# The seam between two phases of a recommender kernel: query term, softmax denominator, exponentials and stores rearranged

## The chip, the cores and the metric

The kernel runs on one core of one Trainium2 chip. The metric is the device time of one execution in microseconds (us); smaller is better. The engines are called as in the profile: PE (TensorE, matmuls), PEld (its weight loads), DVE (VectorE), ACT (ScalarE), POOL (GpSimd) and SP (SyncE, which here only issues DMA transfers).

## The reference, cut to what matters

B is 1024 users, T is 100 steps, all widths are 128.

```python
def gru_step(h, x_t):                        # phase 1: h0 = 0, over 100 steps
    gi, gh = x_t @ gru_Wih.T + gru_bih, h @ gru_Whh.T + gru_bhh
    ...
    h_new = (1.0 - z) * n + z * h
keys = jnp.swapaxes(gru_seq, 0, 1)           # every h
q = jnp.broadcast_to(item_embedding[:, None, :], keys.shape)
feat = jnp.concatenate([keys, q, keys - q, q * keys], axis=-1)
score = _mlp(feat, [(att_W0, att_b0), (att_W1, att_b1), (att_W2, att_b2)], relu)
score = jnp.where(mask[:, :, None] == 1, score, -jnp.inf)
attn = softmax(score, axis=1)[..., 0]        # over the 100 steps
pooled = jnp.einsum('bt,btd->bd', attn, keys)
att_seq = pooled.T[:T]
def augru_step(h, inp):                      # phase 2: over the keys again
    x_t, a_t = inp
    ...
    u = a_t[:, None] * u
    h_new = (1.0 - u) * h + u * h_hat
attention_feature = aug_out[b, sequential_length[b] - 1]
comb = concat([user, item, hist_sum, item * hist_sum, attention_feature])
scores = _mlp(comb, [(ph_W0, ph_b0), (ph_W1, ph_b1), (ph_W2, ph_b2)], sigmoid)
```

The second recurrence needs the softmax over all 100 steps of the first, for its weight `a_t` is a row of `pooled` transposed. So the two phases run one after the other, with a seam where the softmax is finished, the pooled rows are stored and gathered again, and the second recurrence starts.

## The kernel before, in words

Everything is 32-bit floating point. The batch lies in the columns, in two halves of 512 (`HB`), so that a state is a tile of 128 x 512.

**Phase 1** (`gru_phase`) is a Python loop over the steps. In each step both halves do a GRU step (L534 matmuls, four column tiles of 32 at a time), and behind them the attention network works as a pipeline on the keys. `attend(t)` (L700) issues three layers at once on PE for both halves into one pair of PSUM banks `pm`: layer 1 of step t (weights `wk` and `wkq` on the state `hn` and on `kq`, the state times the item), and layers 2 and 3 of the two steps before it (weights `w12` on `mv`). `take(t)` evicts that: DVE adds the item's constant part `q0` to it (L734, tile `f`), ACT applies relu (L739) into `mv`. `q0` was made once by `item_part`, as `wq` times the item plus the biases `bm`. The layers after the last step, t = 100 and 101, have no first layer, and `take` applies relu with the bias straight from PSUM (L741). In `take`, row `SC` of `mv` is the score of step t-2, which two SP transfers per step bring into `s_b`.

**The softmax** is done block by block over the steps; the last blocks (`ENDS`) are 93 to 95, 96 to 97 and 98 to 99. A block has three stages, which `stage()` takes one after the other: `scores(0)`, `tops` (scores of half 1, L786 and L790, then maxima and subtraction, L794 to L800) and `sums` (mask L809, denominator L810 to L814). Between the second and the third stands the exponential on ACT (L806), issued by `exponents()`. In the seam (`banks` filled) the weights of the last two blocks are worked on in PSUM, and `sums` copies them to SBUF (L823) for POOL. `Half.pool(count, eng)` then multiplies keys by weights and adds them up (L626, L636, L637), on POOL for half 0 and on DVE for half 1.

**The seam** is written out by hand after the loop, from `gather_early(4)` on. It interleaves the attention layers of steps 98 and 99 and the two that follow, the `features` (`some(k)`: four matmuls each, L667, then a copy by ACT, L675, and one store of `part_d` per half), the softmax stages and the pooling. At its end DVE multiplies by `used` (L978) and stores to `pooled_d`: columns of steps 0 to 31 first (L982), the rest by SP (L987, half 1) and by ACT (L1410, half 0). The keys of the last rows are stored by `half.store` (L609), 1 MB per half.

A value loaded from DRAM then chooses one of three programs of **phase 2** by branches that every engine takes for itself. Phase 2 (`augru_phase`) works on users sorted by length. Key rows come by indirect gathers on POOL (L188; `load_row(1, 0, k)` for sixteen k, fourteen of them before the branch), the pooled rows by eight more (`gather_weights`, L153). PE transposes keys (L1110), makes the first step's gates (L1030), opens gates (L1127), spreads the first weights (L1053), and then `half_step` alternates between the halves, PE closing and opening gates (L1131, L1127).

There is no planner. Each engine runs its instructions in the order in which the code issues them, and waits for the others by semaphores.

Of the kernel before, what the change touches and what calls it, by code (L numbers as in the profile page):

```python
# [9 lines left out]
F32 = mybir.dt.float32  # L10
# [4 lines left out]
ALU = mybir.AluOpType  # L15
# [4 lines left out]
P = 128  # L20
B = 1024
T = 100
# [61 lines left out]
def kernel(ctx: ExitStack, tc: tile.TileContext, a: dict, out: bass.AP):  # L84
# [114 lines left out]
    def gru_phase(pools):  # L199
# [491 lines left out]
        def attend(t):  # L691

            p = left[t] = [pa.tile([P, HB], F32, tag="a", name="pm") for _ in halves]

            old = [half.mv if t else hist[:, half.cols] for half in halves]
            k_rows = slice(0 if t <= T else 2 * R, P)

            def pack(i, q, w, v, start, stop):
                s = ts(q, R)
                nc.tensor.matmul(p[i][s, :], lhsT=w[:, s], rhs=v, start=start, stop=stop)  # L700

            def first(i, q, j):
                if t < T:
                    w = (wk, wkq)[j][i]
                    pack(i, q, w, halves[i].first[t][j], j == 0 and q != QB[i], j == 1)

            def more(i, q):
                pack(i, q, w12[i][k_rows, :], old[i][k_rows, :], True, q == QA[i] or t >= T)

            for turn in range(2 * NH):  # L710
                i, j = divmod(turn, 2)
                for q in range(2):
                    first(i, q, j)
                if i == 0:
                    for q in range(2, P // R):
                        more((QA, QB)[j].index(q), q)
                else:
                    for q in range(2, P // R):
                        first(QB.index(q), q, j)
# [4 lines left out]
        def take(t):  # L724

            if t < 0:
                return
            p = left.pop(t)
            rows = slice(0 if t < T else 2 * R, P)
            sums = []  # L730
            for half in halves:
                if t < T:
                    sums.append(wp.tile([P, HB], F32, name="f"))
                    nc.vector.tensor_add(sums[-1], p[half.i], q0[:, half.cols])  # L734
            for half in halves:
                half.mv = wp.tile([P, HB], F32, name="mv", bufs=4)
                to, of, bias = half.mv[rows, :], p[half.i][rows, :], bm[half.i][rows, :]
                if t < T:
                    nc.scalar.activation(to, sums[half.i], AF.Relu)  # L739
                else:  # L740
                    nc.scalar.activation(to, of, AF.Relu, bias=bias)  # L741
            s, j = t - 2, soft["j"]
            if s < 0:
                return
            for half in halves:
                nc.sync.dma_start(
                    out=s_bs[NH * (j % 2) + half.i].rearrange("(p r) f -> p r f", r=R)[
                        :, s - blocks[j], :
                    ],
                    in_=half.mv[SC[half.i] : SC[half.i] + 1, :]  # L750
                    .unsqueeze(1)
                    .to_broadcast([1, P // R, HB]),
                )
            if s == blocks[j + 1] - 1:
                softmax()


        def softmax():

            j = soft["j"]  # L760
            b0, b1 = blocks[j], blocks[j + 1]
            n, last = b1 - b0, b1 == T
            rows = n + (1 if j else 0)
            on = later["on"][:, :, b0:b1]
            top_old, den_old = soft.get("top"), soft.get("den")
            e = sp.tile([P, NK, 2 * G + 1], F32, name="e", bufs=3)
            both = e, None
            if banks:

                b = banks["e"].pop()  # L770
                both = e, b[:, : NK * (G + 1)].rearrange("p (k n) -> p k n", n=G + 1)
                e = both[1]
                top_n, den_n = (b[:, NK * m : NK * (m + 1)] for m in range(G + 1, G + 3))
            top = sp.tile([P, NK], F32, name="top", bufs=3)
            den = sp.tile([P, NK], F32, name="den", bufs=3)
            if both[1] is None:
                top_n, den_n = top, den
            soft.update(j=j + 1, top=top, den=den, e=both)

            def scores(i):  # L780
                ks = ts(i, KH)
                if banks:
                    pt = blocked(banks["pt"])
                else:
                    pt = pa.tile([P, KH, R], F32, tag="a", name="pt")
                nc.vector.transpose(  # L786
                    pt, s_bs[NH * (j % 2) + i].rearrange("p (k r) -> p k r", r=R)
                )

                nc.vector.tensor_mul(e[:, ks, :n], pt[:, :, :n], on[:, ks, :])  # L790

            def tops():
                scores(1)
                nc.vector.tensor_reduce(top_n, e[:, :, :n], AX.X, ALU.max)  # L794
                if j:
                    nc.vector.tensor_max(top, top_n, top_old)
                    nc.vector.tensor_sub(e[:, :, n], top_old, top_n)
                    if both[1] is not None:
                        nc.vector.tensor_scalar_min(e[:, :, n], e[:, :, n], 0.0)
                nc.vector.tensor_sub(  # L800
                    e[:, :, :n], e[:, :, :n], top.unsqueeze(2).to_broadcast([P, NK, n])
                )
                soft["exp"] = exponents

            def exponents():
                nc.scalar.activation(e[:, :, :rows], e[:, :, :rows], AF.Exp)  # L806

            def sums():
                nc.vector.tensor_mul(e[:, :, :n], e[:, :, :n], on)  # L809
                nc.vector.tensor_reduce(den_n, e[:, :, :n], AX.X, ALU.add)  # L810
                if j:
                    old = sp.tile([P, NK], F32, name="old")
                    nc.vector.tensor_mul(old, den_old, e[:, :, n])
                    nc.vector.tensor_add(den, den_n, old)  # L814
                if last:
                    nc.vector.reciprocal(den, den)
                    nc.vector.tensor_mul(
                        e[:, :, :rows],
                        e[:, :, :rows],
                        den.unsqueeze(2).to_broadcast([P, NK, rows]),  # L820
                    )
                if both[1] is not None:
                    nc.vector.tensor_copy(both[0][:, :, :rows], e[:, :, :rows])  # L823
                for half in halves:
                    if j:
                        half.todo.append((both, n, None))
                    half.todo += [(both, t - b0, t) for t in range(b0, b1)]

            soft["stages"] += [lambda: scores(0), tops, sums]

        def stage(count=1):
            for _ in range(count):
                if soft["stages"]:
                    soft["stages"].pop(0)()
# [87 lines left out]
        def some(*these):  # L922
            for f in these:
                next(features[f])
# [6 lines left out]
        weights = soft["e"][0]  # L931
        exponents()
        some(0, 1)
        some(2, 3)
        take(T - 1)
        some(2, 3)
        attend(T)
        some(4)
        for half in halves:
            half.transpose(T - 1)  # L940
        stage()
        n = ENDS[-3] - ENDS[-4] + 1
        copy = banks["e"][0][:, : NK * n].rearrange("p (k n) -> p k n", n=n)
        nc.vector.tensor_copy(copy, weights[:, :, :n])
        for half in halves:
            half.todo = [
                ((w[0], copy if w[0] is weights else None), n, t) for w, n, t in half.todo
# [2 lines left out]
        halves[1].pool(1, nc.vector)  # L950
        stage()
        take(T)
        some(4)
        attend(T + 1)
        some(5, 6)
        stage()
        take(T + 1)
        exponents()
        some(5, 6)
        some(7)  # L960
        for half in halves:
            half.store((T - 1) // G)
        halves[1].pool(T, nc.vector)
        stage()
        gather_early(3)
        halves[0].pool(T, nc.gpsimd)
        some(7)
        stage(2)
        exponents()
        stage()  # L970
# [5 lines left out]
        for half in reversed(halves):  # L976
# [6 lines left out]
            later["att", half.i] = [  # L983
                (others[p - 1], t[p * R : (p + 1) * R]) for p in range(1, P // R)
            ]
        for to, t in later["att", 1]:
            nc.sync.dma_start(out=to, in_=t)  # L987

    def augru_phase(pools, widths, alive):

# [415 lines left out]
        gates = [first_step(i) for i in range(NH)]  # L1406
        for i in range(NH):
            load_key(1, i, (FREE_BANK, None)[i])
        for to, t in later["att", 0]:
            nc.scalar.dma_start(out=to, in_=t)  # L1410
        sorted_rows = [gather_weights(i) for i in range(NH)]
        for k in range(14, KH):
            load_row(1, 0, k)
        for i in range(NH):
            load_key(2, i, (FREE_BANK, None)[i])
# [11 lines left out]
        for t in range(1, T):  # L1427
# [6 lines left out]
            for i in range(NH):  # L1434
# [3 lines left out]
                    whole_step(t)  # L1438
                for _ in range(due.pop(0) if due else 0):
                    next(ahead, None)  # L1440
                if t > FIRST[1]:
                    next(more, None)
                if t == FIRST[2]:
# [113 lines left out]
```

## Time and profile before

| | us |
|---|---|
| median of 3 runs | 2017.4 (2016.58 to 2022.05) |
| the profiled execution, its own time | 2009.0 |
| its span in the profile | 2007.1 |
| PE busy | 1983.7 (99%) |
| DVE busy | 1671.7 (83%) |
| POOL busy | 1274.2 (63%) |
| ACT busy | 934.8 (47%) |
| phase 1's last matmul of a GRU step starts | about 1374 |
| phase 2 runs without a hole on PE from | 1432.9 |

The profile shows one execution. Its own time is 8.4 us below the median of the runs, so a sum worked out on the profile is a difference, to be taken from the median. Busy PE is not PE at its peak, but an idle PE is lost time wherever PE is the bound. A line in a timeline gives start, duration, engine, line, operation and tiles; a bracket at its end gives how long the engine was idle before it, and whose end released it. "issue" there means that the profile shows nothing that was waited for.

### The profile page before, as it was taken

What the parts mean: (1) busy time and instruction counts of PE and PEld (TensorE: products, weight loads), DVE (VectorE), ACT (ScalarE), POOL (GpSimd) and SP (SyncE); (2) the same over time, 40 slices, a digit from 0 to 9 for tenths busy, and PEclk for the clock granted to TensorE, in tenths of its full rate; (3) what the DMA queues carried; (4) which work ended last, traced back from release to release, by engine and by line L of the source; (5) the groups of instructions that cost most, each with busy time, mean ns of one, the idle gap of its engine ahead of it and who ended that gap; (6) DMA issues with size and microseconds to landing.
All of it is one profiled execution on the core that took longest, in us unless ns stands there. A gap on an engine that the chain in (4) does not pass through costs nothing. (4 is left out here: it accounts for less than half of the span.)

```text
span 2007.1 us, 41031 instructions
## 1 busy us (share of the span) xinstructions
PE 1983.7 (99%) x15380; PEld 994.6 (50%) x15380; DVE 1671.7 (83%) x3010; ACT 934.8 (47%) x1672; POOL 1274.2 (63%) x1325
## 2 busy tenths in 40 slices
PE   9999999999999999999999999998899999999998
PEld 2334444444444444444444444434444556678997
DVE  7878999887978888888878798998577777888985
ACT  4444454454544454544444454554343444444553
POOL 0233939669796959496896868898774353445331
PEclk9999999999999999999999999999999999999998
DMA  4443333333334434333333333333443343333331
GB/s 125 98 118 92 107 99 106 91 83 106 115 106 109 121 103 125 115 104 102 103 105 106 107 92 107 108 91 94 123 132 99 94 112 95 93 101 99 84 79 32
DMA packets 242075, 204.85 MB, mean 102 GB/s; under 512 B 59506, under 2 KB 204890, under 8 KB 241866
## 3 DMA queue, kind: packets, MB, share of 16 engines
q1 hardware_dynamic: 227514, 169.37, 30.2%
q0 software_dynamic: 12480, 32.04, 5.8%
q8 instruction: 123, 2.02, 0.4%
q10 hardware_dynamic: 1872, 0.72, 0.1%
q14 instruction: 86, 0.70, 0.1%
HBM read 146.01 MB, written 54.41 MB: 100 GB/s over the span
## 5 line engine op out<-in xcount | busy, mean ns | idle before, releaser
L534 PE MATMUL ps<-x,wih 128*32 128x512 f32 x4800 | 616.3, 593 | 0.0
L534 PE MATMUL ps<-hn,whh 128*32 128x512 f32 x4752 | 610.7, 592 | 1.4 <-ACT hn L582 1.4
L534 PEld LDWEIGHTS ps<-x,wih 128*32 128x32 f32 x4800 | 216.1, 110 | 302.0 <-issue 298.7
L534 PEld LDWEIGHTS ps<-hn,whh 128*32 128x32 f32 x4752 | 214.3, 110 | 298.9 <-issue 295.3
L519 POOL TENSOR_TENSOR xm<-x,m 128x512 f32<-128x512 f32 x200 | 234.9, 1174 | 143.2 <-DMA m<-mask_d 142.9
L546 ACT ACTIVATE r<-ps,brz 128x512 f32<-128x512 f32 x200 | 137.7, 689 | 386.3 <-PE ps L534 386.1
L520 POOL TENSOR_TENSOR hist<-hist,xm 128x512 f32<-128x512 f32 x200 | 257.9, 1290 | 15.7
L188 POOL DMA_INDIRECT rows<-keys_d,idx_k x218 | 211.5, 970 | 80.7 <-POOL rows L187 72.5
L637 POOL TENSOR_TENSOR pooled<-pooled,kw 128x512 f32<-128x512 f32 x191 | 245.0, 1283 | 15.0
L636 POOL TENSOR_TENSOR kw<-kt,e 128x512 f32<-128x512 f32 x191 | 206.2, 1080 | 69.7 <-DVE e L809 69.6
L565 ACT ACTIVATE ps<-ps,bih 128x512 f32<-128x512 f32 x200 | 132.4, 662 | 229.4 <-DVE ps L564 229.4
L700 PE MATMUL pm<-hn,wk 128*32 128x512 f32 x1200 | 221.8, 592 | 0.0
L700 PE MATMUL pm<-kq,wkq 128*32 128x512 f32 x1200 | 221.7, 592 | 0.0
L1139 ACT ACTIVATE c<-ph,bh 128x510 f32<-128x510 f32 (+57 forms) x174 | 88.3, 507 | 261.1 <-PE ph L1131 261.0
L554 DVE SCALAR_TENSOR_TENSOR u<-ps,bhh,r 128x512 f32<-128x512 f32 x198 | 147.5, 745 | 71.3 <-PE ps L534 68.6
L700 PE MATMUL pm<-mv,w 128*32 128x512 f32 (+1 forms) x808 | 195.4, 592 | 0.6 <-DVE e L790 0.6
L569 DVE TENSOR_TENSOR d<-hn,ps 128x512 f32<-128x512 f32 x198 | 136.1, 687 | 35.9 <-ACT ps L565 35.7
L564 DVE TENSOR_TENSOR ps<-ps,u 128x512 f32<-128x512 f32 x200 | 140.0, 700 | 25.9 <-remote 4.5
L582 ACT COPY hn<-ps 128x512 f32<-128x512 f32 x200 | 116.6, 583 | 93.5 <-DVE kq L576 91.8
L570 DVE TENSOR_TENSOR d<-ps,d 128x512 f32<-128x512 f32 x200 | 138.4, 692 | 26.0 <-ACT ps L566 11.6
L187 POOL COPY rows<-rest 128x1 f32<-128x1 f32 x202 | 38.4, 190 | 175.4 <-DVE rest L1168 170.0
L571 DVE TENSOR_TENSOR ps<-ps,d 128x512 f32<-128x512 f32 x200 | 139.9, 700 | 6.8
(224 smaller groups left out, 3111.8 us busy)
## 6 DMA issues: line engine op xcount, KB each, us to landing
x<-in_hist_x SPq DMA_DIRECT2D x210, 256.0 KB
keys_d<-kt SPq DMA_DIRECT2D x48, 1024.0 KB
m<-mask_d SPq DMA_DIRECT2D x200, 128.0 KB
rows<-keys_d,idx_k POOLq DMA_INDIRECT x218, 3.0
s_b<-mv SPq DMA_DIRECT2D x200, 8.0 KB
keys_d<-kt SPq DMA_DIRECT2D x32, 64.0 KB
mask_i<-in_mask SPq DMA_DIRECT2D x8, 200.0 KB
part_d<-part SPq DMA_DIRECT2D x2, 400.0 KB
```

The costliest lines, as they stand in the source:

```text
L188: nc.gpsimd.indirect_dma_start(out=r[:, at, :], out_offset=None, in_=keys_d[q], in_offset=bass.IndirectOffsetOnAxis(ap=idx_k[:, k, i : i + ...
L519: nc.gpsimd.tensor_mul(d, x, m)
L520: nc.gpsimd.tensor_add(acc, acc, d)
L534: nc.tensor.matmul(p[ts(q, R), :], lhsT=w[:, g, ts(q, R)], rhs=v, start=(j == 0), stop=(j == len(parts) - 1),)
L546: nc.scalar.activation(r, pr, AF.Sigmoid, bias=brz[:, 0:1])
L554: nc.vector.scalar_tensor_tensor(out=u, in0=ph, scalar=bhh[:, 2:3], in1=r, op0=ALU.add, op1=ALU.mult,)
L564: nc.vector.tensor_add(pi, pi, u)
L570: nc.vector.tensor_mul(d, pz, d)
L571: nc.vector.tensor_add(pi, pi, d)
L636: eng.tensor_mul(d, k, w)
L637: eng.tensor_add(acc, acc, d)
L700: nc.tensor.matmul(p[i][s, :], lhsT=w[:, s], rhs=v, start=start, stop=stop)
```

## The change

1. `attend` for steps 98 and 99 issues, for both halves, the query term too: `wq` on the item, six more matmuls of 32 columns per layer, summed up in `pm`. `take` for these steps drops the DVE addition and applies relu with the bias `bm` straight from PSUM.
2. In `sums` of block 93 to 95 the copy of the weights to PSUM comes ahead of the denominator, which is summed from the copy, and the temporary `old` lies in PSUM. The separate copy after the third stage goes.
3. The seam is put in another order: one feature less ahead of each of attend(100) and attend(101); `exponents()` of block 96 to 97 ahead of `take(101)`; half 1's pooling split so that more of it comes ahead of the last block's scores; POOL's second pooling ahead of the row gathers, which are two there instead of three; the keys' stores after the last feature, which puts them behind the second `part_d` store on SP.
4. The `pooled_d` stores of steps 32 to 99 (six transfers) are issued on SP in step t = 2 of phase 2, three after each half step, instead of three by SP at the end of phase 1 and three by ACT at the start of phase 2.
5. One key row gather more (three instead of two) comes after the pooled rows' gathers.

On the engines' queues: PE 12 matmuls more; DVE two pairs of additions less; ACT the same count without the three transfers; SP three transfers more.

```diff
@@ attend
+            def query(i, *groups):
+                for q in groups:
+                    pack(i, q, wq[i], item[:, halves[i].cols], False, False)
+
             for turn in range(2 * NH):
                 i, j = divmod(turn, 2)
+                if j and T - 2 <= t < T:
+                    query(i, 0, 1)
+                    if i:
+                        query(1, QB[1])
+                        query(0, QB[0])
                 for q in range(2):
                     first(i, q, j)
@@ take
-                if t < T:
+                if t < T - 2:
                     sums.append(wp.tile([P, HB], F32, name="f"))
                     nc.vector.tensor_add(sums[-1], p[half.i], q0[:, half.cols])
...
-                if t < T:
+                if t < T - 2:
                     nc.scalar.activation(to, sums[half.i], AF.Relu)
                 else:
                     nc.scalar.activation(to, of, AF.Relu, bias=bias)
@@ sums
                 nc.vector.tensor_mul(e[:, :, :n], e[:, :, :n], on)
-                nc.vector.tensor_reduce(den_n, e[:, :, :n], AX.X, ALU.add)
+                f, old = e, None
+                if banks and both[1] is None:
+                    b = banks["e"][0]
+                    f = soft["copy"] = b[:, : NK * rows].rearrange("p (k n) -> p k n", n=rows)
+                    old = b[:, HB - NK :]
+                    nc.vector.tensor_copy(f, e[:, :, :rows])
+                nc.vector.tensor_reduce(den_n, f[:, :, :n], AX.X, ALU.add)
                 if j:
-                    old = sp.tile([P, NK], F32, name="old")
-                    nc.vector.tensor_mul(old, den_old, e[:, :, n])
+                    if old is None:
+                        old = sp.tile([P, NK], F32, name="old")
+                    nc.vector.tensor_mul(old, den_old, f[:, :, n])
                     nc.vector.tensor_add(den, den_n, old)
@@ the seam
         some(0, 1)
-        some(2, 3)
+        some(2)
         take(T - 1)
-        some(2, 3)
+        some(2)
         attend(T)
-        some(4)
+        some(3)
...
-        n = ENDS[-3] - ENDS[-4] + 1
-        copy = banks["e"][0][:, : NK * n].rearrange("p (k n) -> p k n", n=n)
-        nc.vector.tensor_copy(copy, weights[:, :, :n])
+        copy = soft["copy"]
...
         take(T)
-        some(4)
+        some(3)
         attend(T + 1)
-        some(5, 6)
+        some(4, 5)
         stage()
+        exponents()
         take(T + 1)
-        exponents()
-        some(5, 6)
-        some(7)
+        some(4, 5)
+        some(6, 7)
+        halves[1].pool(1, nc.vector)
+        stage()
+        halves[0].pool(T, nc.gpsimd)
+        gather_early(2)
+        halves[1].pool(2, nc.vector)
+        some(6, 7)
         for half in halves:
             half.store((T - 1) // G)
-        halves[1].pool(T, nc.vector)
-        stage()
-        gather_early(3)
-        halves[0].pool(T, nc.gpsimd)
-        some(7)
         stage(2)
         exponents()
...
-        for to, t in later["att", 1]:
-            nc.sync.dma_start(out=to, in_=t)
@@ augru_phase
-        for to, t in later["att", 0]:
-            nc.scalar.dma_start(out=to, in_=t)
         sorted_rows = [gather_weights(i) for i in range(NH)]
-        for k in range(14, KH):
+        for k in range(13, KH):
             load_row(1, 0, k)
...
+                if t == FIRST[1] - 2:
+                    for to, of in later["att", i]:
+                        nc.sync.dma_start(out=to, in_=of)
```

## The prediction

> **What bounds the kernel now.** The page's first part comes first: TensorE (PE) is busy nearly all the time, so time can only be won where it is not.
>
> ```profile
> PE 1983.7 (99%) x15380; PEld 994.6 (50%) x15380; DVE 1671.7 (83%) x3010; ACT 934.8 (47%) x1672; POOL 1274.2 (63%) x1325
> ```
>
> Next the table by stage tells where the missing per cent lies: PE (first number after the stretch) is full before 1373 us and after 1433 us, and has its holes in between, where the two phases meet and where the whole edit lies.
>
> ```profile
> 1345.00:1373.00 28.00, 28.00 (x264) 10.24 (x260) 25.95 (x41) 14.91 (x24) 25.17 (x23) 1.00 0.25 73
> 1373.00:1400.00 27.00, 25.82 (x162) 14.90 (x154) 23.47 (x47) 11.85 (x24) 23.14 (x21) 1.00 0.19 57
> 1400.00:1433.00 33.00, 22.34 (x87) 12.59 (x88) 17.25 (x39) 11.21 (x18) 23.77 (x24) 0.84 0.47 118
> 1433.00:1460.00 27.00, 27.00 (x73) 12.79 (x74) 19.37 (x32) 10.05 (x16) 20.19 (x36) 1.00 0.56 170
> ```
>
> So 11.8 us of idle PE are all that can be had. The chain of waits says which wait ends last there: the eighth gather of the pooled rows, then half 1's first state, then PE without a hole to the end.
>
> ```profile
> 1427.23 3.61 DMA att_r<-pooled_d,idx
> ...
> 1431.41 0.71 DVE spare L1064
> ...
> 1432.15 0.70 DVE h_all L1065
> ...
> 1432.89 1.12 PE pr L1131 x2
> ```
>
> The timelines of the engines show what stands just behind that gather, and what leads to it.
>
> ```profile
> 1389.31 1.02 DVE L813 TENSOR_TENSOR old<-den,e 128x32 f32<-128x32 f32 x1
> 1390.37 1.29 DVE L814 TENSOR_TENSOR den<-den,old 128x32 f32<-128x32 f32 x1
> ...
> 1400.16 0.19 DVE L813 TENSOR_TENSOR old<-den,last 128x32 f32<-128x32 f32 x1
> ```
> ```profile
> 1405.47 1.94 PE L1110 MATMUL pk<-ident,rows 128*128 128x128 f32 x8 [6.10 <-issue]
> 1409.13 2.07 PE L1030 MATMUL pu<-k,wu 128*128 128x512 f32 x2 [1.73 <-ACT k L1111]
> ...
> 1424.92 1.16 PE L1053 MATMUL first<-ident,att_r 128*128 128x128 f32 x8 [0.72 <-ACT k L1111]
> ```
> ```profile
> 1403.73 0.23 ACT L806 ACTIVATE last<-last 128x96 f32<-128x96 f32 x1 [4.00 <-DVE last L800]
> 1408.01 1.07 ACT L1111 COPY k<-pk 128x512 f32<-128x512 f32 x2 [4.04 <-PE pk L1110]
> ```
> ```profile
> 1411.35 1.27 POOL L637 TENSOR_TENSOR pooled<-pooled,kw 128x512 f32<-128x512 f32 x1
> ...
> 1418.45 0.95 POOL L153 DMA_INDIRECT att_r<-pooled_d,idx  x1 [2.17 <-DMA pooled_d<-s_b]
> ```
>
> Two chains run to 1432.89. The **data chain**: DVE and POOL finish the softmax and pooling (1414.12 with the last product, L978), the store lands, POOL issues eight gathers at 1.25 us. The **start chain** of the second phase: PE leaves the branch at 1405.47, ACT at 1408.01, and PE works through keys and first gates until 1424.92. Without the gather's wait half 1's weight row (`spare`, PE 1429.94 to 1431.37) would end about 0.4 us sooner; the two chains are that close.
>
> **What the Trainium skill says.** *Runtime: NRT & Kernel Launch*, Instruction fetch mechanics: a taken branch whose target is outside the fetched window forces a DMA fetch first. The trace agrees that the branch costs: PE 6.10 us, ACT at most 4.05 (its last exponential ends at 1403.96). POOL's pause is 2.17. *SBUF — State Buffer*, SBUF: two separate sides: DVE with two SBUF inputs and GpSimd exclude each other for a whole instruction. The trace agrees: L813 with both inputs in SBUF took 1.02 us, ending just after POOL's multiply (1389.19, 1.07 long); with one in PSUM 0.19. *TensorE: Matmul & The Clock Gate*, Part 3: column tiles run side by side, but matmuls start in order. The trace agrees: passes of 0.59 us start every 0.107 us.
>
> **The change part by part.**
>
> *Query on PE.* Each of attend(98) and attend(99) gets six more matmuls. Sixteen take 3.43 us (1346.89 to 1350.32), so six take 1.29 if the four column groups stay full; two of them fall on groups 0 and 1 alone, an extra round of 0.43 more. I take 1.72 each, 3.43 in all. In return DVE loses two pairs of L734 adds (about 1.2 each), and ACT waits for PE instead of DVE. Step by step, before in brackets: attend(98) ends about 1379.5 [1377.8]; `mv` of 98 at 1380.2 to 1381.4, behind the state's copy [1382.69], each activation at 0.63 as the 64-row ones of L741 (bound above 0.69, L546's); features 0 and 1 take 2.9, to 1382.5 [1381.61]; attend(99) 5.15, read from 1388.1 [1386.46, by DVE]; `mv` of 99 ends 1389.35 [1388.42]. So layer 99 is **0.9 later**, not earlier.
>
> *Denominator by PSUM.* L813 and L814 fall from 2.31 to twice 0.19: 1.9 us off DVE; the copy L944 only moves. DVE's start on block 93-95 is 1.2 earlier, and the exponential follows: sums done at about 1386.8 [1391.86], one key pooled to 1388.9.
>
> *Where that stall goes.* Block 96-97 needs `mv` of 99 in `s_b`. Its two SP issues take 0.5 each; landing I take as 2.5, as of the `att_r` gathers (2.4 to 2.6); bounds 1.5 to 3.5, since this trace never lets DVE wait for it. That is 1391.3 and 1391.9, so DVE, five us ahead, now idles 2.4. Then its own 3.04 of scores and maxima: 1394.4 [1396.94].
>
> *Exponentials ahead.* exp of 96-97 at 1394.5 on ACT, then `mv` of take(101), for which attend(101) is ready at about 1394.6 since one feature fewer stands before it: ends 1396.0 [1396.49]. Queued behind it: the feature copies. Behind the maxima DVE has one key (1.45), sums (1.1), two keys (3.6), then scores of 98-99 (3.0): exp at **1403.45** [1403.73]. The pooling put ahead uses up nearly all that was won. Sums 1.95, then seven operations instead of ten, 4.95: 1410.6 [1412.80].
>
> *POOL.* Block 93-95 ends 1394.9; without the three row gathers it waits for block 96-97's weights until 1396.9, five operations of 5.9 to 1402.7, two gathers 2.5, weights of 98-99 at 1405.7, 5.9 to 1411.5 [1412.62]. The last L978 product ends 1412.2 [1414.12], **1.9 earlier**. Three gathers (3.8) and the branch's 2.17 lead to 1417.4; the store, if 4.2 from issue to release again, to 1416.4. So the eight gathers start at 1417.4, 1.0 earlier (up to 2.0 if the pause was all store), and the last lands at 1429.8 [1430.84]. One gather more stands after them (1.25 on POOL), before paced ones that wait for `rest` at 1434: covered.
>
> *Start chain.* Features 4 to 7 now all follow attend(101): PE is through at 1400.1 [1399.37], and leaves the branch at 1406.2 at the same 6.1. ACT leaves it at 1407.7. Both still give the keys' copies 0.2 to 0.3 sooner: `first` at 1424.7, half 1's row from 1429.7, and with 1.05 for its eight passes DVE starts at about 1430.7 [1431.41]. PE pr at **1432.2, 0.7 us sooner**.
>
> *Stores put off.* The keys' two stores (1 MB each) go behind the second `part_d`, from 1397.1 to about 1401. The six `pooled_d` stores (SP 1.88, ACT 1.69 of issue) leave 1414 to 1418 for step t=2, about 1443. On ACT this frees nothing that PE waits for: PE runs gate openings until 1422. On SP they stand before `at` of (4,1), wanted a step later; DVE waits once for rows there (1.10 at 1460.08) under a full PE. I take 0; bounds -1.5 (the first stores land sooner alone) to +1.5 (rows late).
>
> Sum: 0.7 off, on a span of 2007.1 and its own time of 2009.0. The median of the runs shown is 2017.4 (2016.58 to 2022.05), 8.4 above; I subtract from the median: **2016.7**.
>
> **Rivals.** *Faster:* PE's 6.10 is fetch behind the keys' stores, and goes with them. For it: the DMA engines are full from 1398.8 to 1408.4. Against: ACT's branch at 1403.7 then lies in the stores instead, and the gathers bind after about 1.7 us. 2015.7.
> *No change:* `s_b` lands later than 2.5, exp of 98-99 slips past 1403.73, and the start chain loses what the gathers win. 2017.4.
> *Slower:* the keys' stores drain too late. They share SP's queue with the first `pooled_d` stores. At the trace's 9.6 us they drain at 1411, and the stores come at 1411.3 and 1412.2. From a drain after about 1413.2 the gathers slip with it, after 1414.2 they are later than now. A drain at 1417 costs 2.5 us: 2019.9. For it: 1 us of room; against: the rate is measured.
>
> **How the numbers follow.** Chances: forecast 0.50, faster rival 0.20, no change 0.15, slower 0.15. A measurement of this kernel tells about 0.3% from no change, 6.05 us, half of all idle PE in the stage. Faster by that much 0.12 (a quarter of the faster rival, the rest scatter of runs and what I have not seen), slower 0.08 (a third of the slower rival, and scatter), within 0.80. The unknowns reach from -3 to +3 us and the runs themselves spread 5.5: 2011.5 to 2020.5.
>
> **What would show it.** Right: L813 and L814 at 0.19 in block 93-95; DVE idle some 2.4 us before the transposes of 96-97; `mv` of 99 ending near 1389.3; exp of 98-99 near 1403.5; the eight gathers from 1417.4; half 1's pr at 1432.2. Wrong: PE out of its branch below 1404, or the gathers after 1418.5.

## The result, and the profile after

Over 14 executions each on one chip the changed kernel took 2021.78 us (2019.05 to 2025.22) and the kernel before 2019.01 us (2016.58 to 2022.05): a ratio of 1.0014, interval 1.0007 to 1.0021. It is slower by some 2.8 us; two repetitions gave 1.0015 each (below). The profiled execution has a span of 2019.5 us and an own time of 2021.3 us.

The first part of the page shows PE as busy as before:

```profile
PE 1989.4 (99%) x15404; PEld 985.9 (49%) x15404; DVE 1668.6 (83%) x3006; ACT 934.2 (46%) x1672; POOL 1274.9 (63%) x1325
```

In the table by stage (length, then busy time of PE, PEld, DVE, ACT and POOL, then granted clock, DMA share, GB/s) PE has lost its hole before 1400 us, and the one after it has grown:

```profile
1345.00:1373.00 28.00, 28.00 (x264) 10.28 (x260) 26.03 (x41) 15.02 (x24) 25.18 (x23) 1.00 0.25 75
1373.00:1400.00 27.00, 27.00 (x187) 14.93 (x180) 22.38 (x51) 11.87 (x23) 23.92 (x23) 1.00 0.12 39
1400.00:1433.00 33.00, 19.12 (x72) 10.93 (x71) 11.22 (x27) 9.53 (x16) 24.11 (x23) 0.77 0.44 119
1433.00:1460.00 27.00, 25.87 (x72) 12.71 (x73) 16.33 (x26) 9.81 (x15) 13.95 (x24) 0.90 0.50 136
```

The timelines of DVE, PE, ACT and POOL, one after the other, at the places that the prediction named:

```profile
1386.73 0.20 DVE L829 TENSOR_TENSOR last<-den,last 128x32 f32<-128x32 f32 x1
1386.96 0.19 DVE L830 TENSOR_TENSOR den<-den,last 128x32 f32<-128x32 f32 x1
...
1390.99 0.73 DVE L795 STREAM_TRANSPOSE last<-s_b 128x512 f32<-128x512 f32 x1 [1.92 <-DMA s_b<-mv]
```
```profile
1402.94 1.06 PE L1123 MATMUL pk<-ident,rows 128*128 128x128 f32 x8 [2.27 <-issue]
1410.73 2.07 PE L1043 MATMUL pu<-k,wu 128*128 128x512 f32 x2 [6.73 <-ACT k L1124]
```
```profile
1402.76 0.23 ACT L815 ACTIVATE last<-last 128x96 f32<-128x96 f32 x1 [1.72 <-DVE last L809]
1409.60 1.07 ACT L1124 COPY k<-pk 128x512 f32<-128x512 f32 x2 [6.61 <-issue]
```
```profile
1416.08 0.95 POOL L153 DMA_INDIRECT att_r<-pooled_d,idx  x1 [0.36 <-issue]
```

The softmax work went as planned, and so did the gathers, which start at 1416.08 instead of 1418.45. But ACT now stands still for 6.61 us between its last exponential and its first key copy, where it stood for 4.05, while PE's pause, 6.10 before, shrank to 2.27. PE has the first keys ready at once and then waits 6.73 us for ACT. The chain of waits has left the gathers and runs through ACT:

```profile
1402.76 0.23 ACT last L815
1402.99 0.42 ACTq L1497
1403.53 6.00 issue
1409.67 0.42 issue
1410.09 0.60 ACT k L1124
...
1431.99 0.70 DVE first L1077
1432.72 0.70 DVE h_all L1078
...
1440.80 1.12 PE pr L1144 x2
```

From the start of attend(98) to half 1's pr, the stage in which the whole edit lies, this execution took 66.02 us (1374.78 to 1440.80), the one before 58.54 (1374.35 to 1432.89). Not all of these 7.5 us belong to the change: a second profile of the same program (e14, below) has 59.32.

### The profile page after: what moved, and what is told of

It is laid out like the page before. It is cut to its first block, busy times and chain, and to the rows that moved or that the text cites. A ratio compares the mean times of both kernels' runs of the same rounds, so it can differ in the third digit from the quotient of the medians.

```text
span 2019.5 us, 41068 instructions
## 1 busy us (share of the span) xinstructions
PE 1989.4 (99%) x15404; PEld 985.9 (49%) x15404; DVE 1668.6 (83%) x3006; ACT 934.2 (46%) x1672; POOL 1274.9 (63%) x1325
## 4 chain that ended last, share of the span: by engine, by line
PE 95%; DVE 2%; issue 1%; ACT 1%; DMA 1%; SPq 0%; ACTq 0%; DVEq 0%
PE ps L534 49%; PE pm L700 17%; PE ph L1144 4%; PE pr L1144 4%; PE ph L1140 4%; PE pu L1144 4%; PE pu L1140 4%; PE pr L1140 4%; PE pr L1217 0%; PE ph L1217 0%; DMA item<-in_item 0%; PE spare L1066 0%; PE p L1304 0%; PE p L1345 0%; PE pu L1217 0%
## 5 line engine op out<-in xcount | busy, mean ns | idle before, releaser
L534 PE MATMUL ps<-x,wih 128*32 128x512 f32 x4800 | 788.8, 592 | 0.0
L534 PE MATMUL ps<-hn,whh 128*32 128x512 f32 x4752 | 782.9, 592 | 1.4 <-ACT hn L582 1.4
L534 PEld LDWEIGHTS ps<-x,wih 128*32 128x32 f32 x4800 | 236.3, 110 | 306.8 <-issue 277.9
L534 PEld LDWEIGHTS ps<-hn,whh 128*32 128x32 f32 x4752 | 234.3, 110 | 302.0 <-issue 294.9
L700 PE MATMUL pm<-hn,wk 128*32 128x512 f32 x1200 | 260.2, 592 | 0.0
L700 PE MATMUL pm<-kq,wkq 128*32 128x512 f32 x1200 | 260.1, 592 | 0.0
L700 PE MATMUL pm<-mv,w 128*32 128x512 f32 (+1 forms) x808 | 242.4, 592 | 1.4 <-DVE e L799 1.4
```

Of the source, the lines that this page charges most:

```text
L534: nc.tensor.matmul(p[ts(q, R), :], lhsT=w[:, g, ts(q, R)], rhs=v, start=(j == 0), stop=(j == len(parts) - 1),)
```

## The experiments

All times below from a profile are counted from the start of attend(98), since executions drift apart by a microsecond or two before it. "Exit" is the start of ACT's first key copy (`k<-pk`). One column comes from the DMA view: the pages of program that the engines fetch appear there as packets of kind "instruction", and cutting the time around the branch into steps of 0.2 us shows when. The figures here and in the table give the start of the step, so a packet can come up to 0.2 us later. In all 17 profiles a packet of about 8 KB on the queue q14 starts 1.7 to 2.1 us ahead of ACT's exit, and a packet of 16 KB on q8 starts 2.5 to 3.2 us ahead of PE's first transpose in phase 2. The records don't name the engine that a packet is for; that the distance is so nearly the same in every kernel is what ties the one to ACT and the other to PE. The second column gives the time at which the issue of the keys' stores starts.

| kernel | keys' stores issued, us | last exponential ends | then until the packet | ACT's exit | half 1's pr | its distance from the exit | ratio to before |
|---|---|---|---|---|---|---|---|
| before | 22.8 | 29.6 | 2.2 | 33.7 | 58.5 | 24.9 | 1 |
| after | 26.8 | 28.2 | 4.6 | 34.8 | 66.0 | 31.2 | 1.0014 |
| e5, after again | 26.8 | 28.2 | 4.7 | 34.9 | 65.2 | 30.3 | 1.0015 |
| e14, after, third | 26.8 | 28.2 | 4.6 | 34.6 | 59.3 | 24.7 | 1.0015 |
| e1 | 22.3 | 28.2 | 3.2 | 33.4 | 58.6 | 25.2 | 0.9994 |
| e2 | 26.8 | 28.2 | 4.8 | 34.8 | 60.5 | 25.7 | 1.0009 |
| e3 | 27.1 | 30.3 | 5.5 | 37.6 | 63.3 | 25.7 | 1.0014 |
| e4 | 25.9 | 29.6 | 3.4 | 34.8 | 59.7 | 24.8 | 1.0001 |
| e12, e4 again | 25.8 | 29.6 | 3.2 | 34.6 | 59.3 | 24.7 | 1.0004 |
| e11 | 25.9 | 29.6 | 3.4 | 34.7 | 59.6 | 24.8 | 1.0004 |
| e6 | none here | 28.3 | 1.6 | 31.7 | 61.1 | 29.4 | 0.9994 |
| e7 | none here | 31.2 | 1.4 | 34.3 | 62.0 | 27.7 | 0.9996 |
| e8 | 15.1, by ACT | 29.8 | 1.3 | 33.1 | 63.0 | 29.9 | 1.0005 |
| e9 | 15.5 | 29.9 | 1.3 | 32.9 | 58.2 | 25.3 | 1.0001 |
| e10 | 26.8 | 26.9 | 3.0 | 31.8 | 57.5 | 25.6 | 0.9994 |
| e13 | 15.5 | 30.8 | 1.2 | 34.0 | 58.8 | 24.8 | 0.9994 |
| e15 | 22.4 | 27.0 | 3.9 | 32.7 | 58.1 | 25.5 | 0.9999 |

The kernel before took 2008 us beside e1 to e4 and e9 to e15, and 2019 us beside the first comparison and e5 to e8; e5 to e8 ran on another chip than the other experiments. The profile of the kernel before is of the first kind, that of the changed kernel ("after") of the second.

### First round: which part costs

Two theories stood against each other. Stores: put off, the keys' 2 MB fall into ACT's way through the branch. Rest: something else of the change costs.

**e1_keys_back**, the changed kernel with these stores at their old place:

```diff
         take(T + 1)
+        for half in halves:
+            half.store((T - 1) // G)
         some(4, 5)
...
         some(6, 7)
-        for half in halves:
-            half.store((T - 1) // G)
```

> The changed kernel with one edit undone: the keys' two last stores stand again right behind take(101), ahead of the second part_d store on SP. Theory S (stores in the branch): in the changed kernel these 2 MB fill the DMA engines from about 1402 to 1410 us, while ACT fetches phase 2 behind its branch (6.6 us against 4.05), PE waits and its clock falls; with the stores back near 1397 the ACT pause falls to about 4 us and the time to 2017 to 2019, ratio to before 0.999 to 1.000. Theory P (pooled stores in phase 2) and theory Q (query matmuls on PE): no change from the changed kernel, ratio 1.0010 to 1.0018.

Measured 0.9994 (0.9985 to 1.0002): the loss is gone. ACT's pause is 5.16, PE's 4.18. So, in the changed kernel, putting the stores off is needed for the loss.

**e2_pooled_back**, the changed kernel with the six pooled stores where they were:

```diff
+        for to, t in later["att", 1]:
+            nc.sync.dma_start(out=to, in_=t)
...
+        for to, t in later["att", 0]:
+            nc.scalar.dma_start(out=to, in_=t)
```

> The changed kernel with the six pooled_d stores of steps 32 to 99 back at their old places (three by SP at the end of phase 1, three by ACT at the start of phase 2). Theory P: they delay the weight and row loads of phase 2 when issued in step 2; undone, the time falls by the 2.8 us lost, ratio 0.999 to 1.0003. Theories S and Q: ratio stays 1.0010 to 1.002, or rises by up to 1 us since the six stores stand beside the gathers again.

Measured 1.0009 (1.0001 to 1.0018), between the two kernels; it tells little by itself.

**e3_no_query_on_pe**, the changed kernel with DVE adding the query term again:

```diff
-                if j and T - 2 <= t < T:
+                if False:
...
-                if t < T - 2:
+                if t < T:
```

> The changed kernel with the query term of layers 98 and 99 added by DVE again (no extra matmuls, relu without bias from the sum). Theory Q: the 2.6 to 3.4 us of matmuls lie on the path, so the ratio falls to 0.999 to 1.0003. Theories S and P: within 1 us of the changed kernel, 1.001 to 1.002, because DVE waits for s_b anyway.

Measured 1.0014 (1.0008 to 1.0021): the query on PE is not what costs. ACT's timeline in this kernel has the longest pause of all:

```profile
1403.24 0.23 ACT L815 ACTIVATE last<-last 128x96 f32<-128x96 f32 x1 [3.42 <-DVE last L809]
1410.81 1.07 ACT L1124 COPY k<-pk 128x512 f32<-128x512 f32 x2 [7.33 <-POOL kw L636]
```

The POOL multiply named there can hardly be the releaser: here it is the second of its block, in e1 the first, and in e6 the copy (1405.81) starts before the first multiply of that block (1405.86). Elsewhere the same wait is put down to "issue". The packet is what fits in all of them. Against this, e3's time is no longer than the changed kernel's, though its exit is 2.8 us later; more on that below.

**e4_keys_put_off_alone**, the kernel before with the stores put off and nothing else:

```diff
         some(7)
-        for half in halves:
-            half.store((T - 1) // G)
...
         some(7)
+        for half in halves:
+            half.store((T - 1) // G)
         stage(2)
```

> The kernel before with one edit only: the keys' two last stores put off behind the last feature and the second part_d store. Theory S: this alone makes it slower, ratio 1.001 to 1.002, with PE's branch pause down to 2 to 3 us and ACT's up to 6 or more. Theories P and Q: ratio 0.9995 to 1.0005.

Measured 1.0001 (0.9993 to 1.0008): a miss for the stores theory. The pauses moved the way it said (ACT 4.05 to 5.23, where it named 6 or more, PE 6.10 to 2.64), the time did not. Put off by themselves, the stores make no loss that this comparison can tell.

### Second round: without the stores

**e5_after_again** is the changed kernel itself.

> The changed kernel as it is, beside the kernel before on this chip. All theories: ratio 1.0010 to 1.002. Theory S (the keys' stores in flight lengthen the instruction fetch behind the branch): ACT's pause between its last exponential and its first key copy is 6 us or more, PE's pause behind its features 2 to 3. Theory C (PE's clock falls by chance of its windows): the ratio and the pauses are not tied to each other.

Measured 1.0015 (1.0009 to 1.0021).

**e6_after_no_late_keys** and **e7_before_no_late_keys**: no store of the last key rows at the seam, in the changed kernel and in the one before.

```diff
                 elif n == G - 1 and t < T - 1:
                     self.store(q)
+                    if q == (T - 1) // G - 1:
+                        self.store(q, 1)
...
-        for half in halves:
-            half.store((T - 1) // G)
```

> The changed kernel without the two late key stores: the last four steps' key rows are filled from the four steps before, together with those, within the loop (so the output is not the reference's). Theory S: with quiet DMA engines ACT's pause falls from 6.6 to 2 to 3 us, PE's stays near 2.2; the gathers' wait ends last again; 4 to 5 us faster than the changed kernel, ratio to before 0.998 to 0.9993. Theory C: no better than the changed kernel by more than 1 us, ratio 1.0005 to 1.002.

> The kernel before with the same edit: no late key stores, the last four steps' rows filled early from the four before (output not the reference's). Theory S: PE's pause falls from 6.1 and ACT's from 4.05 to 2 to 3 us each, but the gathers still start at about 1418 behind POOL's and DVE's pooling, so little of it reaches the end: ratio 0.9985 to 1.0000. Theory C: 0.9995 to 1.0005 with the pauses unchanged.

Measured 0.9994 (0.9986 to 1.0003) and 0.9996 (0.9988 to 1.0004). With the DMA engines quiet, ACT's pause is 3.38 and 3.06, PE's 2.06 and 2.96. ACT in e6:

```profile
1402.20 0.23 ACT L817 ACTIVATE last<-last 128x96 f32<-128x96 f32 x1 [1.74 <-DVE last L811]
1405.81 1.07 ACT L1124 COPY k<-pk 128x512 f32<-128x512 f32 x2 [3.37 <-issue]
```

Here the two kernels cost the same. So the rest of the change, without the late stores, makes no loss that can be told either; it takes both together. The kernel e7 is no clean control, though: its last exponential came 1.6 us later than in the kernel before.

**e8_keys_early_by_act**, the changed kernel with the stores on ACT's queue, right behind the last transposes, instead of behind the last feature:

```diff
             half.transpose(T - 1)
+            half.store((T - 1) // G, nc.scalar)
```

> The changed kernel with its two late key stores issued by ACT right behind the last transposes (about 1390 us) instead of by SP behind the last feature (1401). Theory S: the 2 MB are through by about 1400, both pauses are 2 to 3 us, ratio 0.998 to 0.9995, less up to 1 us if the issues hold up ACT's layer 100 or the score rows wait among the stores. Theory C: as the changed kernel, 1.0005 to 1.002.

Measured 1.0005 (0.9997 to 1.0013), undecided. The pause is short, 3.24, but the last exponential comes 1.6 us later than in the changed kernel.

### Third and fourth round: order and stores, each both ways

**e9_keys_early_by_sp**, the changed kernel with the stores on SP right behind the loads of `s_b` for layer 99, instead of behind the last feature:

```diff
             half.transpose(T - 1)
+        for half in halves:
+            half.store((T - 1) // G)
         stage()
```

> The changed kernel with the two stores of the last key rows on SP right behind the loads of s_b of layer 99 (about 1390.5 to 1394), so that their 2 MB are through by about 1402, before ACT's last exponential. Theory branch (ACT's leaving of the branch waits for its program to be fetched behind whatever data is in flight): ACT's pause at its first key copy falls from 6.6 to between 3.1 and 4.0 us, PE's stays 2 to 3, and the time goes from 1.0015 to between 0.9985 and 0.9998 of the kernel before. Rival (the loss lies in the new order of exponentials and pooling, not in the stores): ACT's pause falls, but the time stays at 1.001 to 1.002. What may spoil it: s_b of layers 98 to 101 shares the DMA engines with the stores, and the last exponential comes up to 2 us later.

Measured 1.0001 (0.9993 to 1.0009). The pause fell to 3.03 as expected, the time less than expected; what the text gave as a spoiler came true, the last exponential is 1.7 us later.

**e10_old_order_keys_late**, the changed kernel with the order of exponentials and poolings of the one before, the stores still late:

```diff
-        exponents()
         take(T + 1)
+        exponents()
         some(4, 5)
         some(6, 7)
-        halves[1].pool(1, nc.vector)
+        halves[1].pool(T, nc.vector)
         stage()
-        halves[0].pool(T, nc.gpsimd)
         gather_early(2)
-        halves[1].pool(2, nc.vector)
+        halves[0].pool(T, nc.gpsimd)
```

> The changed kernel with the order of exponentials, key poolings and row gathers of the kernel before; query on PE, the denominator by PSUM and both kinds of stores put off stay. Theory branch: the late stores alone cost, so the pause of ACT stays above 5 us and the time at 1.001 to 1.002. Rival order (it takes the early exponentials together with the late stores, since the kernel before with the late stores alone was at 1.0001): 0.9995 to 1.0005.

Measured 0.9994 (0.9987 to 1.0001), though the stores are as late as in the changed kernel. The rival, order, had it. ACT's timeline shows what moved:

```profile
1399.35 0.23 ACT L815 ACTIVATE last<-last 128x96 f32<-128x96 f32 x1 [0.46 <-DVE last L809]
1404.47 1.07 ACT L1123 COPY k<-pk 128x512 f32<-128x512 f32 x2 [4.88 <-POOL kw L636]
```

With the two keys of block 96 to 97 pooled behind the scores of 98 to 99, as in the kernel before, the last exponential ends at 26.9 us instead of 28.2 (before: 29.6). ACT reaches the branch sooner, and the exit is 3.0 us earlier than in the changed kernel, with a pause still of 4.89. Of these 3.0 us, 1.3 are the earlier exponential; the rest is a shorter wait for the packet, 3.0 us instead of 4.6, with the stores issued at the same time. Why it was shorter no run shows.

**e11_both_put_off** (the kernel before with both kinds of stores put off) and **e12_keys_put_off_again** (e4 once more):

```diff
-        for to, t in later["att", 1]:
-            nc.sync.dma_start(out=to, in_=t)
...
+                if t == FIRST[1] - 2:
+                    for to, of in later["att", i]:
+                        nc.sync.dma_start(out=to, in_=of)
```

> The kernel before with both the keys' and the pooled stores put off, and no other part of the change. If it takes both together to lose (each alone moved nothing that could be told: 1.0001 for the keys' stores alone), the time is 1.001 to 1.002. If the loss needs the early exponentials, it is 0.9995 to 1.0006.

> The kernel before with the keys' stores put off, nothing else, once more and beside the others. If the first result of this edit holds: 0.9993 to 1.0008, with ACT's pause near 5.2 us. If the first was chance and the late stores cost by themselves: 1.0008 to 1.0018.

Measured 1.0004 (0.9995 to 1.0012) and 1.0004 (0.9997 to 1.0011): both edits to the kernel before cost under a microsecond by the middle values, none that can be told. The pooled stores add nothing that shows.

**e13_old_order_keys_early** (e10 with the early stores of e9), **e15_old_order_keys_back** (e10 with the stores at their old place) and **e14_after_third** (the changed kernel on the same chip):

> The changed kernel with the old order of exponentials and poolings and with the keys' stores early on SP, right behind the loads of s_b of layer 99. Theory exit (the stage ends about 25 us after ACT leaves the branch, and ACT leaves it at its last exponential plus a fetch of about 3 us when the DMA engines are quiet, of about 5 and more when the keys are in flight): the last exponential 26.5 to 28.5 us after attend(98) starts, exit at 30 to 31.5 (before 33.7), half 1's pr 55 to 57 (before 58.5), the last gather then binding; time 0.9985 to 0.9995. Rival (the order alone made the difference, the fetch does not matter): as the old order with late keys, 0.9987 to 1.0001, and half 1's pr near 57.5.

> The changed kernel with the old order of exponentials and poolings and with the keys' stores at the place that they had before, behind take(101). Theory exit: the stores are in flight from about 1395 to 1405 as in the kernel before, the last exponential is at about 1399.5, so ACT's fetch meets them fully: pause 4.5 to 6, half 1's pr 57 to 58.5, time 0.999 to 1.0. Rival (the order alone): like the other two variants of the old order.

> The changed kernel as it is, beside its two variants on one chip. Theory exit: 1.001 to 1.002, ACT's pause 6.5 to 7.4, exit near 34.8 us after attend(98) starts. If the chip is one of those whose kernel before runs at 2008, half 1's pr lies 25 to 26 us behind the exit (about 60.5); if at 2018, later. Rival (a loss that only some chips show): here within 0.9995 to 1.0005.

Measured 0.9994 (0.9986 to 1.0002), 0.9999 (0.9991 to 1.0008) and 1.0015 (1.0006 to 1.0024). For e13 I missed: the exit came at 34.0, not at 30 to 31.5. The pause was short, 3.23, but DVE waited for the last scores:

```profile
1400.06 0.73 DVE L795 STREAM_TRANSPOSE last<-s_b 128x512 f32<-128x512 f32 x1 [4.37 <-DMA s_b<-mv]
```

The early stores stood ahead of the `s_b` loads of the last block. So the 2 MB were in the way at each place tried in this stage: early they hold up the scores, later the program. That the exit at 34.0 went with a time of 0.9994 does not fit the theory as it stands; the granted clock, below, can account for it.

### What the runs say together

*ACT's pause is its program on the way behind the keys.* In e6, e7, e8, e9 and e13, where the stores have drained or don't exist, the packet starts 1.2 to 1.6 us after the last exponential. In the twelve others, with the stores under way, it takes 2.2 to 5.5 us. The DMA view of two stretches of 0.2 us in which ACT's packet starts, first the changed kernel, then e9 (queue, packets, MB, share of the 16 engines; q1 holds the keys' stores):

```profile
q1 hardware_dynamic: 104, 0.05, 87.8%
q14 instruction: 1, 0.01, 10.3%
```
```profile
q0 software_dynamic: 11, 0.01, 12.5%
q14 instruction: 1, 0.01, 11.9%
```

*The end of the stage follows ACT's exit.* In the rounds in which the kernel before took 2008 us (and in its own profile), half 1's pr lies 24.7 to 25.7 us behind the exit, in twelve profiles, whatever the order and wherever the gathers are.

*Later exits go with longer times.* Of the eleven kernels in those rounds, the five with exits from 31.8 to 34.0 (mean 33.0) have a mean ratio of 0.9996, the six with exits from 34.6 to 37.6 (mean 35.2) one of 1.0008. That is 2.3 us of time for 2.2 us of exit. The single kernels scatter widely about it: e2 and e14 leave when e4, e11 and e12 do (34.6 to 34.8), with 1.0009 and 1.0015 against 1.0001 to 1.0004.

*Much of this scatter is the granted clock of PE.* The record has its mean over every execution. Among executions of one kernel in one round, a mean clock lower by 0.001 goes with 1.15 to 1.33 us more. With one straight line per round, an estimate can be made of what each kernel would take at equal clock, against the kernel before, each within about half a microsecond:

| kernel | e10 | e15 | e9 | e1 | e13 | e12 | e14 | e11 | e2 | e4 | e3 |
|---|---|---|---|---|---|---|---|---|---|---|---|
| ACT's exit | 31.8 | 32.7 | 32.9 | 33.4 | 34.0 | 34.6 | 34.6 | 34.7 | 34.8 | 34.8 | 37.6 |
| us against before, equal clock | -1.0 | -0.3 | 0.1 | 0.0 | 0.9 | 0.9 | 1.5 | 0.7 | 1.0 | 0.6 | 3.4 |

Now the times follow the exits more closely, by about 0.7 us for each us. The executions of e13 had more clock than those of the kernel before (0.9958 against 0.9947); at equal clock it is slower, as its exit says. And the stores put off alone (e4 and e12, and e11 with the pooled ones) do cost 0.6 to 0.9 us.

*What stays open.* The changed kernel is 2.8 us slower; at equal clock it is 1.5 (e14) or 1.0 us (e5), which is about what its exit is later than that of the kernel before, 1.0 to 1.3 us. The other half of the loss goes with a lower clock: its executions had 0.9941 against 0.9947 beside e14, and 0.9912 against 0.9929 beside e5; for the first comparison the clocks of the kernel before are not on record. Whether the change brings the clock down is not shown: e1 and e3, which hold most of the change, had 0.9953 and 0.9951 beside a kernel before at 0.9947.

In the other rounds, those of 2019 us, all five profiles show 27.7 to 31.2 us between exit and pr, a kernel without the change (e7) among them, and the exits don't order the times: e6 leaves 2.6 us before e7 and takes as long. All five have a second stretch at half clock between 1427 and 1439; the twelve other profiles have none there. Two stretches in the form of the table by stage, first from the changed kernel's profile, then from that of the same kernel in e14 (granted clock third from the end):

```profile
1428.40:1438.50 10.10, 7.40 (x23) 4.68 (x22) 2.45 (x4) 1.91 (x3) 0.95 (x1) 0.50 0.09 26
```
```profile
1413.30:1445.00 31.70, 28.35 (x111) 15.29 (x110) 12.55 (x19) 11.83 (x19) 19.61 (x27) 1.00 0.29 82
```

So the excess in that profile, 66.0 us against 59.3, does not lie in the program alone. Whether the kernel before has such a stretch on that chip, no profile shows. Keeping the last key rows in SBUF and storing them well inside phase 2 would take these stores out of the seam; it was not tried. It needs 16 KB of each partition across the change of phase (1 MB per half over 128 partitions).

No kernel here beats the one before by more than the measurement tells: e1, e10 and e13 stand at 0.9994 with intervals that reach 1.0001 or 1.0002. All three lie clear of the changed kernel. At equal clock e10 alone is clearly ahead, by an estimated 1.0 us.

## Why the prediction was wrong

It forecast 0.7 us less, within what can be told; the kernel is 2.8 us slower. Step by step:

- *Query on PE*: `mv` of 99 ended at 1389.67 (forecast 1389.35), and e3 shows no loss from it. Right, though the two layers grew by 0.9 and 0.6 us, not by 1.72 each.
- *Denominator by PSUM*: the two operations took 0.20 and 0.19 (0.19). Right.
- *Where that stall goes*: DVE idled 1.92 us for `s_b` (2.4). Right in place and nearly in size.
- *Exponentials ahead*: the last one started at 1402.76 (1403.45), right as a number. But that the pooling ahead "uses up nearly all that was won" was put down as even; e10 shows that without it the last exponential ends another 1.3 us sooner, and this exponential is the last thing ahead of ACT's branch.
- *POOL*: the last product ended at 1412.34 (1412.2), the gathers began at 1416.08 (1417.4). The branch cost POOL at most 0.36 here, not 2.17: before, that pause was the store's landing. The gathers were 2.4 us earlier, and it was worth nothing.
- *Start chain*: **this is the step that failed.** It left PE "at the same 6.1" and ACT at its 4.05. The stores moved from PE's fetch (q8 packet at 1402.8 before, 1400.2 after, with PE's last feature ending at 1399.37 and 1400.67) to ACT's (1406.2 before, 1407.6 after). PE came out 2.53 us earlier and ACT 1.59 us later (1.16 from the start of the stage), and PE can do nothing without ACT's copy. `first` was forecast for 1424.7 and came at 1427.62; in e14, 51.7 us after the start of the stage, against 50.6 before. That is about the size of the loss at equal clock, 1.0 to 1.5 us. The rest of the 2.8 us goes with the granted clock, for which the prediction had no term, and its cause stays open.
- *Stores put off*: taken at nothing with bounds of 1.5 us either way, for the pooled rows alone. Those bounds held (e11), but the keys' stores had no price of their own outside the slower rival's queue.

The rivals: the faster one had the mechanism, PE's 6.10 is fetch behind the keys' stores, and its own "against" named what happened: ACT's branch then lies in the stores instead. It was priced as a smaller gain, where ACT was the one on the path. The slower rival, stores that hold the first pooled rows, did not occur: the gathers came early. The sign given as "wrong", PE out of its branch below 1404, was the right alarm: it came at 1402.94.

The Trainium skill, *Runtime: NRT & Kernel Launch*, Instruction fetch mechanics, says that each sequencer drives a DMA queue of its own for its program. The prediction used it for the branch and did not follow it: what is fetched by DMA shares the DMA engines with data. *DMA: Bandwidth & Descriptors*, Queues, rings and completion order, says that an engine goes round the queues that have work, a whole packet at a time. One might read a short wait from that, which the page does not state; the runs show waits up to some 4 us above the quiet one, and the measurement decides.

## What to carry to other kernels

At a branch or a change of program between phases, list for each engine when it gets there, what the DMA engines move just then, and who waits for the engine first. A bulk store that is moved off one engine's fetch can land on the next one's, as here; look for a place where the engine that the start hangs on is already through. And work moved ahead of the last instruction before such a branch can delay the branch, even when the sum of the work stays the same. When the differences are as small as here, compare executions at equal granted clock before a cause is sought in the code.

## What the runs showed of the hardware

- Program pages show up in the DMA view. Leaving the branch took ACT 3.0 to 3.4 us with quiet DMA engines and 4.0 to 7.3 us with 2 MB of stores under way; PE 1.8 to 3.0 us where its page was fetched ahead of the stores or without them, and 4.2 to 6.1 where behind (e1 4.18, e15 4.37, before 6.10).
- PE asks for its page early: in the changed kernel the packet starts at 1400.2, before its last feature has ended at 1400.67.
- PE's first pair of matmuls behind its idle time took 2.07 us where later pairs take 1.02, in both kernels; the granted clock there was 0.50 (1402 to 1412 us before, 1405 to 1414 after).
- Within a round of these runs a mean granted clock lower by 0.001, at about 0.994, went with 1.15 to 1.33 us more, by a straight line through its executions.
